# Six PSUM banks for the last batch's logits, and a later place in the program for the weights of later stages

## The chip, the cores and the metric

The kernel runs on one core of a Trainium2 chip. The metric is the device time of one execution in microseconds (us); the times given are medians over runs. The engines are PE (TensorE, with PEld for its weight loads), DVE (VectorE), ACT (ScalarE), POOL (GpSimd) and SP (SyncE, which here only issues DMAs).

## The reference, cut to what matters

Two graph layers over 16 batches of 1024 nodes with 256 features, each layer followed by a layer norm of input plus output.

```python
# layer 0: 4 heads of 64
h = einsum('bnd,hde->bhne', x, W)
e_src, e_dst = einsum(h, a_src), einsum(h, a_dst)            # per edge type
weight = where(adj == t + 1, e_src[t] + e_dst[t])            # adj is 0 or 1 here: one type
attention = softmax(where(adj == 0, -1e9, leaky_relu(weight, 0.01)))
out = head_norm(relu(attention @ h + bias) + h) * ln_gamma + ln_beta
x = layernorm(x + out)
# layer 1: 8 heads of 32
n = layer_norm(x) * gamma1 + beta1                           # query, key and value at once
attn = softmax(where(adj > 0, n @ n.T / sqrt(32), -inf))     # per head
x1 = x + attn @ n
y = x1 + gelu(layer_norm2(x1) @ W1 + b1) @ W2 + b2
x = layernorm(x + y)
```

All arithmetic of the matmuls is in fp32.

## The kernel before

**Two streams.** Layer 0 of a batch and layer 1 of the batch before are written as two Python generators (`layer0`, `layer1`). A loop at the end of `fast_path` takes a step from one or the other. Which one follows from `place`, a progress counter for each stream (batch, work done in it), and from a planner, `Pace`, which keeps a clock for each engine (`free`) and estimates when a tile is written or read. `nc.now()` is the planner's clock of PE. The program is a straight list of instructions without loops on the chip. `manual_schedule(engines={E.PE, E.Activation, E.DVE, E.Pool})` keeps the instructions of these four engines in the order in which they are written; SP is not in the list.

**Chains.** Smaller pieces of work (norms, transposes, the residual) are generators as well, started with `begin(chain, engine, *needs)`. At each `advance()` a chain takes its next step once the planner says that its needs are met: a tile that is written, or a function that returns a time. `complete(chain)` runs the rest of a chain at once. `later_weights` is such a chain. It loads the rows and columns of norms and biases (ten small loads on SP), then, after a pause, the two matrices `w1_sb` and `w2_sb` (1024 KB each, on SP), and after a second pause it folds a norm's scale and shift into them: a subtraction into `b2_r` (DVE), 16 matmuls into a `po` tile (PE), an addition into `b1_sb` and two scalings of `w1_sb` (DVE).

**Layer 0.** `prepare` takes four pairs of row blocks: it transposes `x` and the adjacency, forms `h` with the source and destination terms, and counts 3.25 of work for each pair. `attention0` has 32 steps, over 2 halves of the queries, 4 heads and 4 pairs of key blocks. In a step DVE forms a weight tile (`p<-cb,dinv,mask`, twice 128x512), three steps ahead of its products on PE (32 records of `acc<-v,p` in the trace). Each step counts 1.0. After each pair of heads `after0` runs norms as a chain; with the last pair of a half it loads `xl` and later makes the transposed `nT` for layer 1.

**Layer 1.** `attention1` has 32 steps as well, over 2 halves of the queries, 2 groups of four heads (`quad`) and 8 key blocks. Step i forms four logit tiles of 128x512 on PE (`ps<-nT`), their exponentials on ACT (`p<-ps`), the mask product of step i-1 on DVE (`p<-p,mask`) and the products of step i-3 on PE (two heads as `po<-p,v` and `po<-p,unit`, two as `po<-v,p`). After eight steps `heads_out` copies a result to `oT` on ACT, transposes it on PE through `side_bank` and divides on DVE; the next group needs the same two `po` tiles. `mlp` follows in its own steps.

**PSUM.** Eight banks: a ring of four named `ps` (logits, and the first product of the MLP), two single ones named `acc0` and `acc1` (layer 0 and, during layer 1's attention, the side transposes), and a ring of two named `po`. `bank0` gives out the one of `acc0` and `acc1` that was taken longer ago; layer 0 marks one as busy while it sums products there.

**The last batch.** When layer 0 has no batch left, `place[0]` is set to `B, 0.0`, and layer 1 of the last batch runs alone.

Of the kernel before, what the change touches and what calls it, by code (L numbers as in the profile page):

```python
# [31 lines left out]
F32 = mybir.dt.float32  # L32
# [7 lines left out]
P = 128  # L40
# [136 lines left out]
def fast_path(  # L177
# [24 lines left out]
    nc = Pace(tc.nc)  # L202
    B, N, D = x.shape
    H0, _, HO = w0.shape
# [7 lines left out]
    HALF = 512  # L212
# [7 lines left out]
    QUAD = 4  # L220
# [6 lines left out]
    def ring(name, bufs, **kwargs):  # L227
        return Ring(nc, ctx.enter_context(tc.tile_pool(name=name, bufs=bufs, **kwargs)), bufs)
# [6 lines left out]
    ps_s = ring("ps_s", 4, space=PSUM)  # L235
# [42 lines left out]
    for i, (src, queue, _) in enumerate(terms):  # L278
        for pair in range(H0 // PAIR):
# [3 lines left out]
                    tensor=src.tensor,  # L283
# [31 lines left out]
    def at_time(t):  # L315
        return lambda: t

    def later_weights():
        for t, src in ((lng0_r, lng0), (lnb0_r, lnb0), (g1_r, gamma1), (be1_r, beta1), (b2_r, b2)):
            nc.sync.dma_start(t, bass.AP(tensor=src.tensor, offset=src.offset, ap=[[0, P], [1, D]]))  # L320
        for t, src in ((g1_c, gamma1), (be1_c, beta1), (g2_c, gamma2), (be2_c, beta2)):
            nc.sync.dma_start(t, src.rearrange("(c p) -> p c", p=P))
        nc.sync.dma_start(b1_sb, b1.rearrange("c p -> p c"))
        yield "tensor", at_time(nc.now() + 6.0)
        nc.sync.dma_start(w1_sb, w1.rearrange("(c p) f -> p c f", p=P))
        nc.sync.dma_start(w2_sb, w2.rearrange("(c p) d -> p c d", p=P))
        yield "tensor", at_time(nc.now() + 24.0)

        nc.vector.tensor_sub(b2_r, b2_r, be1_r)

        pb = ps_o.tile([P, FC], F32, name="po")
        for f in range(FC):
            for c in range(DC):
                nc.tensor.matmul(
                    pb[:, f : f + 1],
                    w1_sb[:, c, f * P : (f + 1) * P],
                    be2_c[:, c : c + 1],
                    start=c == 0,
                    stop=c == DC - 1,
                )  # L340
        yield "vector", pb
        nc.vector.tensor_add(b1_sb, b1_sb, pb)
        for c in range(DC):
            nc.vector.tensor_scalar(w1_sb[:, c, :], w1_sb[:, c, :], g2_c[:, c : c + 1], None, op0=OP.mult)
# [25 lines left out]
    def bank0(shape, dtype=F32):  # L370
        i = min((i for i in range(2) if not banks0[i]["busy"]), key=lambda i: banks0[i]["taken"])
        for chain in banks0[i]["readers"]:
            complete(chain)
        banks0[i].update(readers=[], taken=1 + max(bank["taken"] for bank in banks0))
        return ps_a.tile(shape, dtype, f"acc{i}"), banks0[i]
# [40 lines left out]
    def uses(chain, tile):  # L416
        users.setdefault(tile, []).append(chain)
# [13 lines left out]
    def begin(chain, engine, *needs):  # L431
        for n in needs:
            if not callable(n):
                uses(chain, n.tensor.name)
        chains.append([chain, engine, needs])
# [10 lines left out]
    def advance():  # L446
        for _ in range(2):
            for item in list(chains):
                if item in chains and when(item[2]) <= max(nc.now(), nc.free[item[1]]):
                    run(item)  # L450
# [7 lines left out]
    def complete(chain):  # L458

        for item in list(chains):  # L460
            if item[0] is chain:
                while item in chains:
                    run(item)
# [258 lines left out]
    def attention1(half, mask, rinv, half_done):  # L722

        steps = [(n, quad, jb) for n in range(NH) for quad in range(H1 // QUAD) for jb in range(NB)]

        def exponentials(n, quad, jb):
            keys = slice(jb % BPH * P, (jb % BPH + 1) * P)
            of_keys, of_queries = half(jb // BPH)[2], half(n)[2]
            tiles = [ps_s.tile([P, HALF], F32, name="ps") for _ in range(QUAD)]

            nc.together(tiles)
            for e in range(QUAD):
                q = slice(e * HD, (e + 1) * HD)
                nc.tensor.matmul(tiles[e], of_keys[q, quad, keys], of_queries[q, quad, :], start=True, stop=True)
            nc.together(tiles)  # L740
            ps = []
            for e in range(0, QUAD, PAIR):
                p = eight.tile([P, PAIR, HALF], F32, name="p")
                for i in range(PAIR):
                    nc.scalar.activation(p[:, i, :], tiles[e + i], AF.Exp, scale=SCALE1)
                ps.append(p)
            return ps

        def masked(n, quad, jb, ps):
            for p in ps:  # L750
                nc.vector.tensor_mul(p, p, mask[n][:, jb, None, :].to_broadcast([P, PAIR, HALF]))

        def products(quad, jb, ps, moved, held):
            values = half(jb // BPH)[1][:, jb % BPH, :, :]
            for e in range(PAIR):
                hd = quad * QUAD + e
                for at, v in ((e, values[:, hd, 0:HD]), (PAIR + e, unit)):
                    nc.tensor.matmul(
                        moved[at * Q : (at + 1) * Q, :], v, ps[0][:, e, :], start=jb == 0, stop=jb == NB - 1
                    )  # L760
            for e in range(PAIR):
                hd = quad * QUAD + PAIR + e
                for q in range(BPH):
                    for at in range(0, P, Q):
                        nc.tensor.matmul(
                            held[at : at + Q, q, e, :],
                            ps[1][:, e, q * P + at : q * P + at + Q],
                            values[:, hd, :],
                            start=jb == 0 and e == 0 and q == 0,
                            stop=jb == NB - 1 and e == PAIR - 1 and q == BPH - 1,  # L770
                        )

        LAG = 3
        ready = {}

        def logits_ready():
            return ps_s.ready("ps", QUAD)

        def outs_ready():
            return ps_o.ready("po", 2)  # L780

        for i in range(len(steps) + LAG):
            if i < len(steps):
                ready[i] = exponentials(*steps[i])
                advance()
            if 0 <= i - 1 < len(steps):
                masked(*steps[i - 1], ready[i - 1])
                advance()
            if i < LAG:
                yield 1.0, logits_ready  # L790
                continue
            n, quad, jb = steps[i - LAG]
            if jb == 0:
                moved = ps_o.tile([P, HALF], F32, name="po")
                held = ps_o.tile([P, BPH, PAIR, HD + 1], F32, name="po")
            products(quad, jb, ready.pop(i - LAG), moved, held)
            if jb == NB - 1:
                if quad == 0:
                    o = one.tile([P, BPH, D], F32, name="o0")
                chain = heads_out(n, quad, moved, held, o, rinv)  # L800
                begin(chain, "vector", held, moved, o)
                if quad == H1 // QUAD - 1:
                    half_done(n, o, chain)
            yield (2.5, logits_ready, *ready.get(i - LAG + 1, ()), *([outs_ready] if jb == NB - 1 else []))
# [139 lines left out]
    place = [[0, 0.0], [0, 0.0]]  # L944
# [63 lines left out]
    for i in range(3):  # L1008
        load_adj(i)
    load_blocks(0)  # L1010
    weights_of_later = later_weights()
    begin(weights_of_later, "tensor", at_time(3.0))
    streams, needs, which = [layer0(), layer1()], [(), ()], 0
    while any(streams):
        (b0, done0), target = place[0], wanted()
# [464 lines left out]
```

## Time and profile before

| | us |
|---|---|
| median of 3 runs | 3459.49 |
| lowest, highest | 3459.29, 3473.02 |
| the profiled execution | 3472.71 |
| its span, first to last instruction | 3470.9 |
| PE busy in it | 3321.2 |
| DVE busy | 2982.8 |
| ACT busy | 1937.3 |
| POOL busy | 418.9 |

A matmul of fp32 leaves two records in the trace, so 16 matmuls show as 32. [...] In a row such as `acc<-w0e,xT` the tile written stands ahead of the arrow and the tiles read behind it, with the digits of names left out: `b_r` is `b2_r`, `w_sb` is either matrix. Nearly all instructions bear line L61, that of the helper that records them for the planner, so groups are told apart by tiles. The brackets at the end of a line give the idle time of that engine before it and what ended it. The granted clock of PE is a share of full speed.

### The profile page before, as it was taken

Reading aid. Unit: us, or ns where it says so; the run is one execution under the profiler, and the core shown is the slowest. Engines: PE = TensorE matmul, PEld = TensorE weight load, DVE = VectorE, ACT = ScalarE, POOL = GpSimd, SP = SyncE. Lnnn points to the kernel's source line nnn. Section 1 sums busy time; section 2 is a strip of 40 time slices with the busy share of each in tenths; the row PEclk is TensorE's granted clock in tenths of the full one; section 3 lists DMA queues with packets and bytes.
Section 4 is the critical chain, followed back from the end, with each engine's and each line's share of the span. In section 5 each row is a group of like instructions: output and inputs, shape, how many; then the busy total and the mean of one; then the engine's idle time right before and its main releaser. Section 6 shows DMA issues by size and latency. Waiting matters only on the chain.

```text
span 3470.9 us, 141029 instructions
## 1 busy us (share of the span) xinstructions
PE 3321.2 (96%) x64161; PEld 2259.7 (65%) x64161; DVE 2982.8 (86%) x5262; ACT 1937.3 (56%) x4192; POOL 418.9 (12%) x424
## 2 busy tenths in 40 slices
PE   5799999999999999999999999999999999999998
PEld 5458576675856758576585766757667585765846
DVE  5898898988979898898988989889898888989873
ACT  2563846547375573745638466473655737466363
POOL 1102011010110101101020110101101011010200
PEclk9899999999999999999999999999999999999999
DMA  5211202011020111202112020120201112020000
GB/s 135 50 22 37 47 25 58 15 44 40 28 59 21 41 34 33 56 18 58 23 35 48 24 57 18 41 43 27 60 20 40 37 31 59 20 54 10 26 3 14
DMA packets 95727, 131.30 MB, mean 38 GB/s; under 512 B 10384, under 2 KB 61584, under 8 KB 95120
## 3 DMA queue, kind: packets, MB, share of 16 engines
q1 hardware_dynamic: 75104, 87.58, 8.2%
q0 software_dynamic: 18432, 33.56, 6.7%
q8 instruction: 504, 8.26, 1.0%
q10 hardware_dynamic: 1584, 1.05, 0.1%
q14 instruction: 103, 0.84, 0.1%
HBM read 138.68 MB, written 17.04 MB: 45 GB/s over the span
## 4 chain that ended last, share of the span: by engine, by line
PE 72%; DVE 20%; ACT 5%; issue 2%; DMA 0%; POOL 0%; ACTq 0%; POOLq 0%; DVEq 0%
PE po L61 28%; PE ps L61 25%; PE acc L61 19%; DVE p L61 15%; ACT p L61 2%; DVE o L61 1%; DVE x L61 1%; ACT sq L61 1%; DVE st L61 1%; DVE z L61 1%; ACT mask L61 1%; ACT hb L61 1%; DMA w0e<-in_L_gnn_W_dram 0%; DVE v L61 0%; ACT z L61 0%
## 5 line engine op out<-in xcount | busy, mean ns | idle before, releaser
L61 ACT ACTIVATE p<-ps 128x512 f32<-128x512 f32 x2048 | 1061.9, 615 | 403.5 <-PE ps L61 374.8
L61 DVE TENSOR_TENSOR p<-p,mask 128x1024 f32<-128x1024 f32 x1024 | 1187.4, 1219 | 11.9 <-ACT p L61 11.9
L61 DVE SCALAR_TENSOR_TENSOR p<-cb,dinv,mask 128x512 f32<-128x512 f32 x1024 | 711.7, 746 | 0.1
L61 PE MATMUL ps<-nT 32*128 32x512 f32 x4096 | 687.1, 655 | 2.2 <-ACT p L61 2.2
L61 ACT ACTIVATE hid<-ps,b_sb 128x256 f32<-128x256 f32 x512 | 242.6, 474 | 794.9 <-PE ps L61 793.7
L61 PEld LDWEIGHTS po<-v,p 128*32 128x32 f32 x32768 | 395.5, 110 | 335.3 <-issue 287.1
L61 PE MATMUL acc<-v,p 128*64 128x65 f32 x16384 | 563.1, 227 | 33.6 <-DVE p L61 15.8
L61 PEld LDWEIGHTS acc<-v,p 128*64 128x64 f32 x16384 | 517.0, 140 | 114.4 <-issue 55.6
L61 PE MATMUL po<-p,v 128*32 128x512 f32 x2048 | 553.6, 616 | 0.0
L61 PE MATMUL po<-p,unit 128*32 128x512 f32 x2048 | 553.1, 615 | 0.0
L61 PE MATMUL ps<-yT,w_sb 128*128 128x256 f32 x2048 | 489.8, 385 | 0.0
L61 PE MATMUL po<-w_sb,hid 128*128 128x256 f32 x2048 | 474.6, 384 | 0.0
L61 PEld LDWEIGHTS po<-w_sb,hid 128*128 128x128 f32 x2048 | 382.1, 190 | 54.0
L61 PEld LDWEIGHTS ps<-yT,w_sb 128*128 128x128 f32 x2048 | 376.0, 190 | 51.1
L61 PE MATMUL po<-v,p 128*32 128x33 f32 x32768 | 391.1, 198 | 13.5 <-issue 9.6
L61 PEld LDWEIGHTS ps<-nT 32*128 32x128 f32 x4096 | 227.3, 187 | 104.9 <-issue 41.7
L61 PEld LDWEIGHTS po<-p,v 128*32 128x32 f32 x2048 | 78.6, 109 | 332.1 <-issue 174.6
L61 POOL TENSOR_TENSOR r<-v,mhalf 128x1 f32<-128x1 f32 (+1 forms) x192 | 157.9, 831 | 706.4 <-DVE v L61 624.5
L61 DVE TENSOR_TENSOR z<-acc,bias_r 128x256 f32<-128x256 f32 x128 | 54.2, 424 | 183.5 <-ACT hb L61 183.3
L61 PE MATMUL acc<-w0e,xT 128*128 128x264 f32 x512 | 152.1, 421 | 38.4 <-DVE z L61 23.0
L61 POOL DMA_DIRECT2D ak<-in_adj_dram x128 | 69.7, 545 | 974.6 <-PE acc L61 962.0
L61 POOL TENSOR_TENSOR r<-v1s,mhalf 128x4 f32<-128x4 f32 x32 | 61.5, 1923 | 992.0 <-DVE v1s L61 992.0
(108 smaller groups left out, 2745.6 us busy)
## 6 DMA issues: line engine op xcount, KB each, us to landing
ak<-in_adj_dram POOLq DMA_DIRECT2D x128, 256.0 KB, 3.9
cb<-esr SPq DMA_DIRECT2D x64, 512.0 KB
xk<-in_x_dram SPq DMA_DIRECT2D x64, 256.0 KB
xl<-in_x_dram SPq DMA_DIRECT2D x32, 512.0 KB
out_dram<-z SPq DMA_DIRECT2D x128, 128.0 KB
w_sb<-in_L_gnn_W_dram SPq DMA_DIRECT2D x2, 1024.0 KB
esr<-rows SPq DMA_DIRECT2D x64, 4.0 KB
v<-in_L_gnn_a_src_dram SPq DMA_DIRECT2D x2, 320.0 KB
```

The source lines that it names most:

```text
L61: return method(*args, **kwargs)
```

## The change

Three edits. First, a counter `turn` over the logit tiles of `attention1`: while layer 0 has no batch left, tiles with turn 4 and 5 out of six come from `bank0`, the others from the ring `ps` as before. Second, the chain `later_weights` begins when the work counter of layer 0 is above 16, in place of the planner's time 3.0. Third, its two matrices follow when that counter is above 24, in place of 6 planner microseconds after the small loads. The folding still follows 24 planner microseconds after the matrices.

```diff
@@ later_weights
         nc.sync.dma_start(b1_sb, b1.rearrange("c p -> p c"))
-        yield "tensor", at_time(nc.now() + 6.0)
+        yield "tensor", lambda: 0.0 if place[0][1] > 24.0 else math.inf
         nc.sync.dma_start(w1_sb, w1.rearrange("(c p) f -> p c f", p=P))
         nc.sync.dma_start(w2_sb, w2.rearrange("(c p) d -> p c d", p=P))
         yield "tensor", at_time(nc.now() + 24.0)
@@ attention1
+        turn = [0]
+
+        def logits_tile():
+
+            turn[0] = (turn[0] + 1) % 6
+            if place[0][0] == B and turn[0] >= QUAD:
+                return bank0([P, HALF])[0]
+            return ps_s.tile([P, HALF], F32, name="ps")
+
         def exponentials(n, quad, jb):
             keys = slice(jb % BPH * P, (jb % BPH + 1) * P)
             of_keys, of_queries = half(jb // BPH)[2], half(n)[2]
-            tiles = [ps_s.tile([P, HALF], F32, name="ps") for _ in range(QUAD)]
+            tiles = [logits_tile() for _ in range(QUAD)]
@@ fast_path
     weights_of_later = later_weights()
-    begin(weights_of_later, "tensor", at_time(3.0))
+    begin(weights_of_later, "tensor", lambda: 0.0 if place[0][1] > 16.0 else math.inf)
```

## The prediction

> **What bounds the kernel now.** I read the busy shares first, then busy time by stage, then the timelines of the two stretches that the change touches. PE is busy 96% of the span and leads the chain that ended last with 72%, so a microsecond taken from PE where it runs alone comes off the end.
>
> ```profile
> PE 3321.2 (96%) x64161; PEld 2259.7 (65%) x64161; DVE 2982.8 (86%) x5262; ACT 1937.3 (56%) x4192; POOL 418.9 (12%) x424
> PE 72%; DVE 20%; ACT 5%; issue 2%; DMA 0%; POOL 0%; ACTq 0%; POOLq 0%; DVEq 0%
> ```
>
> Batches 1 to 14 run both layers interleaved and the change leaves their code alone. Two places differ. In the **head** (0 to 122 us) layer 0 of batch 0 runs by itself: DMA to 23 us, a PE-ACT-DVE chain without DMA waits to 49 us, then attention bound by DVE (70.58 us busy of 76). In the **tail** (3286 to 3402 us) layer 1's attention of the last batch runs by itself. Stage rows: us, then busy time of PE, PEld, DVE, ACT, POOL, then granted clock, DMA share, GB/s.
>
> ```profile
> 0.00:23.00 23.00, 1.94 (x12) 1.64 (x12) 4.42 (x18) 2.98 (x4) 3.02 (x10) 1.00 0.82 171
> 49.00:125.00 76.00, 55.28 (x1085) 50.63 (x1086) 70.58 (x136) 7.13 (x14) 8.56 (x5) 0.78 0.08 25
> 3325.00:3332.00 7.00, 5.00 (x89) 2.40 (x92) 4.25 (x6) 2.18 (x6) 0.00 (x0) 0.76 0.01 2
> 560.00:565.00 5.00, 5.00 (x81) 2.12 (x79) 5.00 (x10) 3.86 (x9) 0.00 (x0) 0.50 0.01 3
> ```
>
> In the tail, the timeline of the weight loads for the logits, and of ACT, shows two steps (start, duration, engine):
>
> ```profile
> 3336.55 0.32 PEld L61 LDWEIGHTS ps<-nT 32*128 32x128 f32 x8
> 3339.19 0.45 PEld L61 LDWEIGHTS ps<-nT 32*128 32x128 f32 x6
> 3339.83 0.29 PEld L61 LDWEIGHTS ps<-nT 32*128 32x128 f32 x2 [0.20 <-ACT p L61]
> 3342.44 0.32 PEld L61 LDWEIGHTS ps<-nT 32*128 32x128 f32 x8
> ...
> 3337.72 2.07 ACT L61 ACTIVATE p<-ps 128x512 f32<-128x512 f32 x4 [1.19 <-PE ps L61]
> 3340.35 2.07 ACT L61 ACTIVATE p<-ps 128x512 f32<-128x512 f32 x4 [0.56 <-PE ps L61]
> ```
>
> Steps alternate: 3339.19 - 3336.55 = 2.64 us, then 3342.44 - 3339.19 = 3.25 us. In the long one the fourth logit tile waits until ACT has read the same bank of the step before (ACT ends at 3339.79, the load starts at 3339.83). The short one has no wait and is PE's own work. ACT needs 2.07 us per step and DVE (two masks) 2.36, both less than 2.64.
>
> [...]
>
> **Part 1, six banks.** It removes a wait and adds no instruction. Six tiles in turn put two spare banks between steps: the first two tiles of step i+1 find free banks, the last two need exponentials 0 and 1 of step i. Those end 1.16 + 2 x 0.52 = 2.2 us after step i's logits begin (1.16 is 3337.72 less 3336.55), before PE arrives at 2.64. So each step costs PE's 2.64. From step 4 on, read off the starts of the exponentials, there are 24 intervals inside the four runs of eight steps: 20.29 + 20.29 + 21.31 + 8.52 = 70.41 us. 24 x 2.64 = 63.36, plus 1.3 for eight transposes of the finished half inside the third run (0.66 per four), is 64.7: **-5.7 us**. Between runs (7.36, 7.23 and 5.89 us) PE stands until ACT has copied `oT`, which follows that step's four exponentials in ACT's order: nothing gained. The side transposes there take a bank that the logits now share, but the exponentials of that bank come earlier on ACT than `oT`: covered by that wait. If it weren't, about 1 us at each of three boundaries. Steps 0 to 3 (3286 to 3303) are bound by ACT (12.88 of 17 us) with PE in waits; six banks let logits run ahead by a step. I take -0.6, bounds 0 and -2. The last three products and the MLP (3398 to 3463) use other banks: 0. Part 1: **-6.3**, bounds -2 (PE is held by something else) and -9.
>
> **Part 2, the loads.** The program writes 12 loads on SP after a later step. The layer-0 counter reaches 13 in preparation (4 x 3.25), 14 at the start of attention and one more per step, so ten small loads stand behind step 2 and the two matrices of 1024 KB behind step 10. Does SP issue them later? SP's timeline says probably not:
>
> ```profile
> 22.51 1.10 SPq L61 DMA_DIRECT2D w_sb<-in_L_gnn_W_dram  x2
> 23.72 4.78 SPq L61 DMA_DIRECT2D xk<-in_x_dram  x2
> 28.59 0.42 SPq L61 DMA_DIRECT2D xl<-in_x_dram  x1
> 30.86 0.61 SPq L61 DMA_DIRECT2D esr<-rows  x1
> 34.57 0.38 SPq L61 DMA_DIRECT2D xk<-in_x_dram  x1
> ```
>
> `xl` is written in `after0` behind step 15, yet it is issued at 28.59, before the first `esr`, which the program writes in preparation; the `xk` at 34.57 belongs to batch 1. `manual_schedule` fixes the order of PE, ACT, DVE and POOL, not SP: a load goes out when what it overwrites is free. The weights overwrite nothing, so I expect them where they were, from 8.21 us: **0**. If they do move, they pass three `xk`, `xl`, four `esr` and two `cb` on SP. Then 5 x 0.131 MB leave the first 23 us, 17% of what moved there (171 GB/s x 23 us = 3.9 MB), or up to 3.8 us; I price it at -3.5. The cost then is covered: at 252 GB/s (the rate of 23 to 49 us) 2.1 MB take 8 us from about 69 us on, and what could queue behind them is first needed later: the last `cb` near 102 us, `xl` at 92.9. `lng_r`, issued near 54, is read at 76.37.
>
> **Part 3, the compute behind the loads.** `b2_r`, 16 matmuls (32 records) into `po`, `b1_sb` and two scalings of `w1_sb` move with the generator. Now they sit after step 2:
>
> ```profile
> 54.24 4.62 PE L61 MATMUL po<-be_c,w_sb 128*128 128x1 f32 x32
> ...
> 55.45 0.42 DVE L61 TENSOR_TENSOR b_r<-b_r,be_r 128x256 f32<-128x256 f32 x1
> 58.90 0.16 DVE L61 TENSOR_TENSOR b_sb<-b_sb,po 128x8 f32<-128x8 f32 x1 [3.03 <-PE po L61]
> 58.98 1.41 DVE L61 TENSOR_SCALAR w_sb<-w_sb,g_c 128x1024 f32<-128x1024 f32 x2
> ...
> 94.86 2.00 PE L61 MATMUL acc<-v,p 128*64 128x65 f32 x32 [2.51 <-DVE p L61]
> 101.47 1.78 PE L61 MATMUL acc<-v,p 128*64 128x65 f32 x28 [4.60 <-DVE p L61]
> ```
>
> DVE, the bound of this stage, loses 0.42 + 3.03 + 0.16 + 1.41 = 5.0 us. The new place is 24 planner us behind step 10; steps average (122.6 - 49.7)/32 = 2.3 us in the trace, so 10 or 11 steps on: steps 20 to 22. Counting 32 records per step, step 22 starts at 94.86 and step 23 at 101.47, with PE idle 4.60 between, while DVE does the row statistics. The 4.62 us of matmuls fit that hole, and DVE comes to the addition after 102.39, when they are done. The 3.03 go, the 1.99 of DVE work stay: **-3.0**. If they fall into a dense run of products instead (80.72 to 86.25), the wait stays and PE is late: bounds -3 and +2. Later products wait for DVE's weights as before.
>
> **Sum.** -6.3 + 0 - 3.0 = -9.3. The profiled execution took 3472.7 (span 3470.9 and 1.8 around it), which gives 3463.4. It lies 13.2 above the median of 3459.5; against the median, which I forecast, 3450.2.
>
> **Rivals.** [...] Starts of `r<-v1s` lie 208.1 us apart in batches such as 2528.24 to 2736.34 and 211.7 in others[...]. The profile's 14 such intervals exceed 208.1 by 33 in all.
> (a) *Clock, fast side*: a shifted head puts fewer batches in the long state. With the profile's 13.2 taken off, the median run has 20 us left over the floor; all gone gives 3430, half 3440. For: neighbouring batches differ without different work. Against: two of three runs agree within 0.2 us.
> (b) *Clock, slower than before*: [...] To lose 0.5% against 3459.5 after gaining 9.3, 26.6/3.6 = 7.4 batches must join the 5.6 (20/3.6) in that state: it decides only from 13 of 14, at 3477; all 14 give 3480.
> (c) *SP follows the program after all*: -3.5 more, 3446.7.
> (d) *The banks give little*, the tail being held by DVE's masks three steps back: -2 in place of -6.3, 3454.5. Against it: the short step shows no such wait.
>
> **Numbers.** Forecast 0.50 (own range 3445 to 3456), (a) 0.22, (b) 0.08, (c) 0.10, (d) 0.10. About 0.5% (17.3 us) is what a measurement of this kernel can tell from no change: below 3442.2 or above 3476.8. Faster takes most of (a) and the low ends of the forecast and (c): 0.28. Slower is most of (b): 0.05. Same 0.67. For eight in ten I leave out the ends of (a) and (b): 3433 to 3465.
>
> **What would show it.** Logit loads of the tail 2.64 us apart without alternation and ACT's idle before `p` even: part 1 right; 2.94 on average: wrong. `w_sb` issued by 24 us: loads not moved; after 50: (c). The `po<-be_c,w_sb` matmuls near 97 us and no 3 us wait before `b_sb`: part 3 right. Batch spacing other than a mix of 208 and 212 us would mean that the order of the middle changed, which I exclude; a total off by over 15 us with these right points to the clock.

## The result, and the profile after

| | before | after |
|---|---|---|
| median of 13 runs each, same chip, us | 3463.56 | 3446.72 |
| lowest, highest | 3457.18, 3473.62 | 3436.66, 3456.58 |
| the profiled execution | 3472.71 | 3455.47 |
| its span | 3470.9 | 3453.7 |

The ratio is **0.9948, 95% interval 0.9934 to 0.9963**: 18 us less, by the interval 13 to 23. The range of the prediction holds the time, but its forecast of 9.3 us less lies below this interval: the gain was about twice as large. The two profiled executions, cut at four events that both have, show where 17.2 us went (us):

| stretch | before | after | difference |
|---|---|---|---|
| start to the first `acc<-w0e,xT` | 23.04 | 21.68 | -1.4 |
| from there to the first `acc<-v,p` (preparation) | 26.67 | 26.71 | 0.0 |
| from there to the first `r<-v1s` (rest of the head) | 155.92 | 152.79 | -3.1 |
| from there to the last batch's first logits load (middle) | 3080.66 | 3076.80 | -3.9 |
| from there to the end (tail) | 184.61 | 175.72 | -8.9 |

In the page, PE's busy time fell by 8.4 us, of which 5.8 lie in the tail's attention (102.3 to 96.5 us for the same matmuls), and its share of the chain of waits did not move:

```profile
PE 3312.8 (96%) x64161; PEld 2252.1 (65%) x64161; DVE 2981.3 (86%) x5262; ACT 1935.6 (56%) x4192; POOL 418.6 (12%) x424
PE 72%; DVE 20%; ACT 5%; issue 2%; DMA 1%; POOL 0%; SPq 0%; POOLq 0%; ACTq 0%; DVEq 0%
```

The attention stage of the head by busy time, in the column order of before (us, then PE, PEld, DVE, ACT, POOL, clock, DMA share, GB/s). DVE's work in it is the same 70.5 us; the stage is 3.2 us shorter.

```profile
47.70:120.50 72.80, 54.27 (x1086) 48.51 (x1087) 70.46 (x136) 7.13 (x14) 8.34 (x5) 0.81 0.09 25
```

**The tail's logits** now come at an even pace: from step 4 on, none of their weight loads waits for an exponential any more. First two weight loads, then ACT (the timelines of after):

```profile
3300.07 0.18 PEld L61 LDWEIGHTS acc<-nT 32*128 32x128 f32 x1
3302.70 0.18 PEld L61 LDWEIGHTS ps<-nT 32*128 32x128 f32 x1
...
3298.60 1.57 ACT L61 ACTIVATE p<-ps 128x512 f32<-128x512 f32 x3 [0.63 <-PE acc L61]
3301.22 0.60 ACT L61 ACTIVATE p<-acc 128x512 f32<-128x512 f32 x1 [0.56 <-PE ps L61]
3303.85 0.60 ACT L61 ACTIVATE p<-ps 128x512 f32<-128x512 f32 x1 [0.56 <-PE ps L61]
```

Steps start 2.62 and 2.63 us apart, where 2.63 and 3.25 alternated, and ACT waits 0.56 to 0.63 us for PE each time.

**The loads** did not move on SP: the small ones still go out from 8.57 us, the matrices at 21.77; only one `xk` is now ahead of them.

```profile
8.57 0.34 SPq L61 DMA_DIRECT2D lng_r<-in_L_gnn_ln_gamma_dram  x1
21.21 0.52 SPq L61 DMA_DIRECT2D xk<-in_x_dram  x1
21.77 0.98 SPq L61 DMA_DIRECT2D w_sb<-in_L_gnn_W_dram  x2
```

**The folding of the weights** did move, and the 3.03 us wait ahead of `b_sb` is gone. The matmuls end at 91.1, and DVE comes to the addition at 96.12:

```profile
86.92 4.19 PE L61 MATMUL po<-be_c,w_sb 128*128 128x1 f32 x32
...
93.39 0.42 DVE L61 TENSOR_TENSOR b_r<-b_r,be_r 128x256 f32<-128x256 f32 x1
96.12 0.15 DVE L61 TENSOR_TENSOR b_sb<-b_sb,po 128x8 f32<-128x8 f32 x1
```

**The boundaries between runs of eight steps**, from ACT's timeline of after. The first is as before: the four exponentials of step 11, the copy of `oT`, and 4.87 us of idle until step 12. The third is not: the exponentials of step 28 start 0.11 us after the copy ends.

```profile
3313.67 0.62 ACT L61 COPY oT<-po 128x512 f32<-128x512 f32 x1
3319.15 1.08 ACT L61 ACTIVATE p<-ps 128x512 f32<-128x512 f32 x2 [4.87 <-PE acc L61]
...
3366.01 0.62 ACT L61 COPY oT<-po 128x512 f32<-128x512 f32 x1
3366.74 1.58 ACT L61 ACTIVATE p<-ps 128x512 f32<-128x512 f32 x3
```

### The profile page after: what moved, and what is told of

The parts are those of the page before. It is cut to its first block, busy times and chain, and to the rows that moved or that the text cites. A ratio compares the mean times of both kernels' runs of the same rounds, so it can differ in the third digit from the quotient of the medians.

```text
span 3453.7 us, 141035 instructions
## 1 busy us (share of the span) xinstructions
PE 3312.8 (96%) x64161; PEld 2252.1 (65%) x64161; DVE 2981.3 (86%) x5262; ACT 1935.6 (56%) x4192; POOL 418.6 (12%) x424
## 4 chain that ended last, share of the span: by engine, by line
PE 72%; DVE 20%; ACT 5%; issue 2%; DMA 1%; POOL 0%; SPq 0%; POOLq 0%; ACTq 0%; DVEq 0%
PE po L61 28%; PE ps L61 24%; PE acc L61 20%; DVE p L61 15%; ACT p L61 2%; DVE o L61 1%; DVE x L61 1%; ACT sq L61 1%; DVE st L61 1%; DVE z L61 1%; ACT mask L61 1%; ACT hb L61 1%; DVE v L61 0%; ACT z L61 0%; DVE hb L61 0%
## 5 line engine op out<-in xcount | busy, mean ns | idle before, releaser
L61 ACT ACTIVATE p<-ps 128x512 f32<-128x512 f32 x2006 | 1042.2, 616 | 384.1 <-PE ps L61 341.5
L61 PE MATMUL ps<-nT 32*128 32x512 f32 x4012 | 676.3, 655 | 0.0
L61 PEld LDWEIGHTS ps<-nT 32*128 32x128 f32 x4012 | 220.1, 186 | 98.0 <-issue 41.3
```

Of the source, the lines that this page charges most:

```text
L61: return method(*args, **kwargs)
```

## The experiments

My theory after the comparison: the banks gave the whole tail, the folding gave 3 us of the head, and the rest (start and middle) is chance. The rivals are written into what was expected of each run. All runs are cut at the same events (us; "head" is first `acc<-v,p` to first `r<-v1s`; preparation, left out here, takes 26.7 to 28.7 us):

| kernel | first `acc<-w0e,xT` | head | middle | tail |
|---|---|---|---|---|
| before | 23.04 | 155.92 | 3080.66 | 184.61 |
| banks alone (`e1_banks`) | 21.90 | 155.82 | 3073.90 | 173.30 |
| weights alone (`e2_weights`) | 23.40 | 152.59 | 3068.00 | 183.06 |
| after | 21.68 | 152.79 | 3076.80 | 175.72 |
| after again (`e8_again`) | 21.67 | 152.76 | 3069.90 | 173.51 |
| five tiles (`e3_five`) | 21.23 | 151.52 | 3066.93 | 176.59 |
| banks for 4 steps (`e4_startup`) | 22.59 | 152.62 | 3070.96 | 180.87 |
| folding earlier (`e7_dense`) | 21.05 | 152.68 | 3062.51 | 174.29 |
| loads on ACT's queue (`e5_loads_act`) | 15.83 | 152.83 | 3056.60 | 172.45 |
| the same, timed (`e10_loads_timed`) | 15.94 | 152.69 | 3059.82 | 175.28 |
| `oT` copied first (`e6_copy_first`) | 21.24 | 151.77 | 3073.30 | 168.04 |
| both of these (`e9_both`) | 16.06 | 152.35 | 3069.50 | 168.05 |

**The two parts apart.** For the banks alone:

```diff
-        yield "tensor", lambda: 0.0 if place[0][1] > 24.0 else math.inf
+        yield "tensor", at_time(nc.now() + 6.0)
-    begin(weights_of_later, "tensor", lambda: 0.0 if place[0][1] > 16.0 else math.inf)
+    begin(weights_of_later, "tensor", at_time(3.0))
```

> The six banks alone; the weights' generator starts at 3.0 and goes on after 6.0, as in the kernel before. Theory: the two parts are independent, and the banks give what the profiles show in the tail, so from the first logits load of the last batch to the end of the span 175.7 us (before: 184.6), with logits loads 2.63 us apart; the head up to the first r<-v1s stays at 205.6 us, with the 3.0-us wait ahead of b_sb. Time 9 us (0.26%) below the kernel before. Rival: [...]180 or so here and 4 to 5 us.

Measured: ratio 0.9946 (0.9926 to 0.9966), head and tail as in the table, a wait of 3.30 us ahead of `b_sb`. For the weights alone:

```diff
-            turn[0] = (turn[0] + 1) % 6
+            turn[0] = (turn[0] + 1) % 4
```

> The places of the weights' generator alone; logits take four tiles in turn. Theory: the head up to the first r<-v1s takes 201.2 us (before: 205.6), of which 3.0 is the wait ahead of b_sb and 1.3 the earlier first product (21.7 against 23.0 us), because one xk goes ahead of the two matrices on SP; the tail stays at 184.6 us. Time 4.5 us (0.13%) below the kernel before. Rival: the earlier first product was chance of one execution, then it is at 23.0 here and the head gains 3.0 to 3.2 us only.

Measured: 0.9984 (0.9970 to 0.9998). Head and tail belong each to their part. The rival of the first run, a tail of 180 or so, is not met: all tails with six tiles in turn throughout lie at 175.7 or below. The first product came at 23.40 with the weights moved and at 21.90 without, so its 1.4 us between the two profiles was chance, as the rival had it. The ratio of the banks alone is lower than the expected 9 us would give (0.9974), and its interval leaves that value out: 18.7 us less, of which tail, start and preparation of its profile hold 11.2. The rest is not explained; the sum of the total below comes back to it.

**How many tiles.**

```diff
-            turn[0] = (turn[0] + 1) % 6
+            turn[0] = (turn[0] + 1) % 5
```

> The kernel after with five tiles in turn in place of six (one of the two acc banks). Theory: a step's logits need the exponential that read the same bank, here 1 to 3 of the step before for its last tiles; the third ends 1.16 + 3 x 0.52 = 2.72 us after the step began, so steps are 2.72 to 2.75 us apart (six: 2.63, four: 2.94 on average), and the seven intervals of the first run of eight steps make 19.0 to 19.3 us (six: 18.5, four: 20.3). Rival: any step that takes a tile of the step before waits for all of it, then the alternation of 2.64 and 3.25 stays and the run makes 20.3. Second rival: one spare bank is enough, 18.5.

Measured: 19.12 us in the first run (its first interval, 3.07, still belongs to the start) and 18.82 in the second. Of five steps, two take 2.77 us and three 2.63. ACT's timeline of this kernel:

```profile
3286.66 2.07 ACT L61 ACTIVATE p<-ps 128x512 f32<-128x512 f32 x4 [0.56 <-PE ps L61]
3289.43 0.60 ACT L61 ACTIVATE p<-acc 128x512 f32<-128x512 f32 x1 [0.70 <-PE ps L61]
3292.05 0.60 ACT L61 ACTIVATE p<-ps 128x512 f32<-128x512 f32 x1 [0.56 <-PE ps L61]
```

The expected interval of 2.72 to 2.75 for every step was not met, and that the mean of 2.69 lies near it proves nothing. But the reader is the right one. In each step of 2.77 us the fourth head's weights are loaded 0.16 us behind the first head's, in the others 0.02: that is the 0.14 lost. This late load comes 0.05 us after the third exponential of the step before, which ends 2.74 us after that step began. A step that follows one of 2.77 begins after that end and has nothing to wait for, and every fifth step takes its spare tile last and needs only the second exponential. The expectation speaks of one `acc` bank; in fact `bank0` still gives out both in turn, and what the edit shortens is the return of a `ps` bank, from six tiles to five.

**The start of the tail.** The two `acc` banks for steps 0 to 3 alone:

```diff
-            if place[0][0] == B and turn[0] >= QUAD:
+            if few and place[0][0] == B and turn[0] >= QUAD:
...
+            few = (n, quad) == (0, 0) and jb < 4
```

> The kernel after, but the two acc banks are used for the first four steps of the last batch alone; from step 4 on four tiles in turn. Theory: the start gained 2.6 us (first logits load to that of step 4: 16.7 before, 14.1 after) by the banks, so 14.1 here; runs of seven intervals 20.3 us as before; the boundary between steps 27 and 28 is 5.9 us again, since it was the free tiles that let those logits go ahead of the transposes (2.7 us after); first logits load to the end 182.0 us. Rival: the start gained by the clock or by what PE still had of layer 0, then 16.7 here or a value in between; and the boundary of 2.7 us came from an earlier change of the order, then 2.7 here too.

Measured: steps 0 to 4 (starts of the exponentials) 13.50 us, against 16.73 before and 14.14 in `e8_again`; up to step 5, where the variant's banks run out, 16.9 against 19.4 and 16.8. From step 5 on the first run is as before; boundary three 5.90 us, tail 180.87. The start's gain is the banks'. PE's timelines show it: the logits of step 3 wait for an exponential in before, so that what follows starts at 3298.38, 12.1 us after the first logits; in after it is 9.2 (3277.98 to 3287.14):

```profile
3294.92 3.53 PE L61 MATMUL ps<-nT 32*128 32x512 f32 x8 [1.51 <-ACT p L61]
3298.38 1.97 PE L61 MATMUL acc<-ident,sq 128*128 128x128 f32 x8
...
3287.14 1.06 PE L61 MATMUL po<-p,v 128*32 128x512 f32 x1
```

Boundary three is the banks' as well: with four tiles PE has `acc<-ident,oT` ahead of step 28's logits, and waits; in after the logits come first (PE's timelines of `e4_startup`, then of after):

```profile
3365.86 0.66 PE L61 MATMUL acc<-ident,oT 128*128 128x128 f32 x4 [2.37 <-ACT oT L61]
...
3365.58 0.70 PE L61 MATMUL ps<-nT 32*128 32x512 f32 x3
3366.68 0.66 PE L61 MATMUL acc<-ident,oT 128*128 128x128 f32 x4
```

With five tiles that boundary is 5.90 us as well. That the planner, which writes this order, found six tiles ready sooner than `oT`, is argued from the order; it wasn't tried by itself.

**The middle.** The same kernel again:

> The kernel after once more, unchanged, for the middle of the span (first r<-v1s to the first logits load of the last batch), whose order of instructions none of the edits touches: 3080.7 us before, 3076.8 after, 3066.9 to 3073.9 in the four runs of variants. Theory: [...]differs from one execution of the same kernel to the next, so it will be off 3076.8 by 3 us or more here, while the stage in the head stays at 152.0 to 153.0 and the tail at 173 to 177. Rival: each kernel has a middle of its own[...], then 3076.8 within 0.5 us.

Measured: 3069.90, so 6.9 us off with nothing changed, while the head moved by 0.03 and the tail by 2.2. Over the twelve profiles the middle takes 3056.6 to 3080.7 us. The 3.9 us by which before and after differ there prove nothing.

**Where the folding stands.**

```diff
-        yield "tensor", at_time(nc.now() + 24.0)
+        yield "tensor", at_time(nc.now() + 13.0)
```

> The kernel after with 13.0 in place of 24.0 in the last yield of the weights' generator: the 16 matmuls into po come about five steps earlier, into a run of products with only weights of DVE between them, and b_r, b_sb and the scaling of w_sb stand one behind another on DVE. Theory: what the new place saved is that the statistics of a half stand between the matmuls and the addition; without them DVE waits 2.5 to 3.5 us before b_sb again, and the stage from the first attention-0 product to the first r<-v1s makes 155 to 156 us as with the early place (now 152.6). Rival: the early place cost because the pipeline had only begun, a later one is free anywhere: no wait over 0.5 us and 152.6.

Measured: a wait of 0.65 us and a head of 152.68. My theory fell and the rival was nearly right in its numbers, though not in its reason. PE's and DVE's timelines say why:

```profile
77.30 1.35 PE L61 MATMUL acc<-v,p 128*64 128x65 f32 x32 [1.37 <-DVE p L61]
78.58 5.87 PE L61 MATMUL po<-be_c,w_sb 128*128 128x1 f32 x32
...
83.41 0.42 DVE L61 TENSOR_TENSOR b_r<-b_r,be_r 128x256 f32<-128x256 f32 x1
84.48 0.16 DVE L61 TENSOR_TENSOR b_sb<-b_sb,po 128x8 f32<-128x8 f32 x1 [0.65 <-PE po L61]
```

PE comes to the folding's matmuls at 78.58 and DVE to the subtraction `b_r` at 83.41, so PE has a lead of 4.8 us. The matmuls take 5.87 and the subtraction 0.42, and what is left, 0.65, is the wait. At the early place the lead was only 1.2 us (54.24 and 55.45 in before), and of 4.62 us of matmuls 3.03 were left. In after the lead is 6.5 us (86.92 and 93.39), more than the 4.19 that the matmuls take there. What counts is how far PE is ahead, not what stands between on DVE.

**The loads, really moved.** In the generator, five times:

```diff
-        nc.sync.dma_start(...)
+        nc.scalar.dma_start(...)
```

> The kernel after, but the generator's twelve loads are issued from ACT's queue, whose order is fixed, in place of SP's; so they really go out behind step 2 (about 50 us) and no longer from 8 us. Theory of the prediction's rival (c): 0.66 MB or more leave the first 23 us, and the first acc<-w0e,xT product comes 2 to 3.5 us earlier than the 21.2 to 23.4 us that six executions with the loads in front show: 18.5 to 20. Rival: the start is held by the loads of the layer-0 weights and attention vectors on their own queues and by DVE's twelve small steps on them, then 21 to 22.5 as now. In both, the stage from the first attention-0 product to the first r<-v1s stays at 151.5 to 152.8 us.

Measured: the small loads now go out from 40.72 us, and the first product comes at 15.83 us, with 3426.15 us for the one execution. That is the prediction's rival (c) as a mechanism, and 6 us in place of 3.5. DVE's and PE's timelines in the repeat of it:

```profile
15.00 0.39 DVE L61 TENSOR_TENSOR z<-w0e,xl 128x128 f32<-128x128 f32 x1
15.94 2.25 PE L61 MATMUL acc<-w0e,xT 128*128 128x264 f32 x4 [5.05 <-issue]
```

In before, DVE reaches that `z<-w0e,xl` at 22.10 and has waited 3.61 us for the attention vectors' DMA. That was the last of three waits: 2.72 us for `w0e`, 0.85 for `v` and these 3.61, all for loads from ACT's queue, and none of the three is left in the repeat. So in this kernel the small loads in front on SP delayed loads on ACT's queue, and the first product by about 6 us. By what way they did so is not shown. Which of the ten small loads does it (five rows of 128 KB, five with packets of 4 bytes) was not tried. The repeat, timed:

> The kernel with the twelve loads on ACT's queue again, now timed. Theory: 6.4 us less than the kernel after from the head (first product at 15.8 us again), so about 23 us (0.67%) below the kernel before; the 3426.15 us of its one execution had a middle of 3056.6 us, the shortest seen, which is chance and does not return in the median. Rival: with the head shifted this way the middle stays short, then the median is near 3430, 34 us below before. Second rival: the early first product was chance, then it is past 20 us here and the gain is that of the kernel after, 17 us.

Measured: 0.9936 (0.9918 to 0.9954), median 3438.37, first product at 15.94. The theory holds; the middle was short again (3059.82), but 3069.50 in the third kernel with these loads.

**The boundaries.**

```diff
                 begin(chain, "vector", held, moved, o)
+                if place[0][0] == B:
+                    run(chains[-1])
```

> The kernel after with one more change: in the last batch the chain heads_out runs its first part (the copy of oT) as soon as it is begun, so on ACT the copy stands ahead of the next step's four exponentials and not behind them. Theory: at the boundaries behind steps 11 and 19 PE stands until that copy (2.62 us of idle before acc<-ident,oT); the copy can go as soon as the products end, so the transposes start right behind the logits of step 11, and the boundaries shrink from 5.9[...] to 3.3 us, like the third one, which stays; first logits load to the end 5 us less (about 169), the time 5 us below that of the six banks. Rival 1: PE then waits for DVE, which divides held before it masks the next step's weights (3.6 us of DVE work in such a step): 4.2 to 4.5 us a boundary, 3 us in all. Rival 2: an exponential that comes 0.6 us later delays the masks, and what a boundary gains is lost in the next step: nothing gained.

Measured: 0.9930 (0.9906 to 0.9955), tail 168.04, first boundary 4.45 us, second 3.24 (the step behind it 0.5 longer), third 3.28. PE's and ACT's timelines at the first:

```profile
3306.95 0.62 ACT L61 COPY oT<-po 128x512 f32<-128x512 f32 x1
3308.82 0.66 PE L61 MATMUL acc<-ident,oT 128*128 128x128 f32 x4 [1.16 <-ACT p L61]
```

The theory holds at the second boundary. The first lies in the range of rival 1, but the 1.16 us left there are a wait for ACT, not for DVE: the transposes take a bank whose logits ACT still has to read. That is the cost of the shared bank that the prediction had set at nothing as long as the copy's wait covers it.

**Both together.**

> The two edits that gained put on the kernel after together: the twelve loads on ACT's queue (first acc<-w0e,xT product at 15.8 us in place of 21.2 to 23.4) and the copy of oT ahead of the exponentials (first logits load to the end 168.0 us in place of 173.3 to 175.7). Theory: they lie 3 ms apart and add up: first r<-v1s at 195 us, tail 168 us, and with a middle of 3057 to 3077 us a span of 3420 to 3440; the time 12 us below the kernel after, about 30 us (0.85%) below the kernel before. Rival: the early first product was chance of one execution; then it is past 20 us here, and the time is that of the copy alone, 24 us (0.7%) below before.

Measured: **0.9909 (0.9892 to 0.9927)**, median 3432.26, first product 16.06, tail 168.05. The two stretches are as short as in the two kernels apart, so the gains add up. This version is faster than before, and its interval lies below that of after (0.9934 to 0.9963).

## Why the prediction was right, and where it was too small

Sizes are taken from before and `e8_again`, where the first two boundaries have equal lengths (7.36 and 7.23 us), so that the granted clock there (in before 0.76 at 3325 to 3332 us and 0.72 at 3354 to 3360) does not blur the sum.

- **Part 1, the 24 intervals: right.** 70.41 us became 18.47 + 18.42 + 20.50 + 7.89 = 65.28: -5.1 for the -5.7 predicted. The third run is short of it: there the finished half's four scalings and two `yT` copies stand between its exponentials on ACT.
- **Part 1, steps 0 to 3: mis-sized.** -2.6 for -0.6, outside the bounds of 0 and -2. I had called the stretch ACT-bound from ACT's busy time (12.88 of 17 us), a share that left 4 us open. But in before PE stopped at the tiles of steps 1 to 3 until exponentials freed them, and everything behind them on PE stopped too: these logits held it for 12.1 us, in after for 9.2.
- **Part 1, boundaries: wrong for one of three.** "Nothing gained" held for the first two. The third went from 5.89 to 3.28 us, -2.6, because with the six tiles another order was written: I had taken the order of the tail as fixed. The 1 us for a shared bank was rightly covered, and showed where `e6_copy_first` removed its cover.
- The ends of the tail (before step 0's exponentials and from step 31 on) differ by 0.8 us, which no run explains; over the twelve profiles the last of them takes 75.0 to 76.5 us. Sum of the tail: -5.1 - 2.6 - 2.6 - 0.8 = -11.1, for -6.3.
- **Part 2: right.** The loads stayed. The price on rival (c) was too low: nine profiles with the loads in front have the first product at 22.0 us on average, three without at 15.9, so 6 us in place of 3.5. The step that failed is the price by share of bytes, which took the rate as given. In `e10_loads_timed` 3.4 MB come before the first product at 15.94 us, 215 GB/s, against 3.9 MB at 171 GB/s before. At 171 GB/s the 0.5 MB fewer would be worth 3 us; the other 4 of these 7.1 us (an estimate from the two rates) came with the higher rate, and why the rate rose is open.
- **Part 3: right in size, by another place.** -3.1 for -3.0. The matmuls came to 86.92, not into the hole at 97, and the wait went because PE was 6.5 us ahead there. The bound that in a dense run the wait stays did not hold in `e7_dense`, with a wait of 0.65 us.
- **The total.** The parts give about -14 with the terms corrected, inside the interval of -13 to -23. The 4 us up to the measured 18 stay open: executions of one kernel differ by more, and rivals (a) and (b) can be neither shown nor ruled out as a share of it. They are not peculiar to this kernel: in all six timed kernels the time fell by 2.5 to 7.5 us more than the stretches outside the middle account for, with the one profile of before as the base. Either that profile is untypical there, or the middles became shorter; no run decides it. The median before in the comparison is also 4.1 us above the one the forecast started from; on that base the forecast was 3454.3. So the 3450.2 came within 3.5 us of the median by luck in part: a base too low by 4.1 us hid about half of what the sum lacked.

## What to carry to other kernels

Cost a bank by its last reader: the spare banks bring the step down to PE's own time once the reader in question ends before PE returns. Here the step took 2.94 us on average with four tiles in turn, 2.69 with five and 2.63 with six. Where a planner writes the order, freeing a resource can also change the order (here the third boundary went from 5.89 to 3.28 us with it), and the boundaries must be priced as well as the steady steps. Where an engine stands waiting in the order written, what is behind it waits too (PE came past the logits of steps 0 to 3 after 12.1 us in before, after 9.2 in after): read the start of a stage from that engine's waits, not from the busy share of another. Loads written later are not loads issued later (on SP they still went out from 8.57 us); look at the queue's timeline, and if nothing holds them, put them on a queue whose order is kept (on ACT's they went out from 40.72 us).

## What the runs showed that was not expected

One and the same middle was 6.9 us longer in one execution than in another, a good third of what the change gave. In all twelve traces ACT, DVE and POOL run their instructions of the middle in the same order. In the middles of six of them (before, after and its repeat, `e2_weights`, `e5_loads_act`, `e7_dense`) DVE is busy for 2721.5 to 2722.7 us, PE for 2997.4 to 3010.3, most in the longest and least in the shortest. Over whole executions the time goes with the mean granted clock: in the 49 runs of before that stand beside the experiments the clock goes from 0.984 in the shortest (3447.27 us) to 0.977 in the longest (3480.65), with a correlation of -0.84. One batch of it, in the kernel after and in its repeat (busy time of the stretch, columns as above):

```profile
831.12:1042.93 211.81, 206.18 (x4010) 140.13 (x4009) 185.69 (x328) 120.86 (x263) 26.06 (x27) 0.98 0.16 37
832.90:1040.96 208.06, 204.56 (x4010) 138.99 (x4009) 185.61 (x328) 120.80 (x263) 26.05 (x26) 0.99 0.16 38
```

The counts and DVE's work are the same; the mean clock is 0.98 and 0.99, and the first takes 3.75 us longer. In the clock records of after, 0.50 was granted for 6.83 us of its batch here (from 977.49 us on) and for 3.41 us of the next one, which takes 208.02 us. No edit here could be judged from the middle. Nor is the clock shown to be all of it: before and after each had 81.9 us at 0.50 in the middle, and their middles differ by 3.9 us. What sets these stretches is not shown either.

And ten early loads, 0.66 MB in all, cost the first product 6 us, although the DMA engines were only 82% busy in the first 23 us of before and of after.
